# A decoder layer on one core: sixteen states of 32 channels per scan step, their sum in quarters of PSUM, and a convolution folded into four weight matrices

## The chip, the cores and the metric

The kernel runs on one core of a Trainium2 chip. A core has five engines, each with its own instruction queue that is worked in order: TensorE (PE; its weight loads are shown apart as PEld), VectorE (DVE), ScalarE (ACT), GpSimd (POOL) and SyncE (SP), which in this kernel only issues transfers. SBUF and PSUM both have 128 partitions; TensorE writes only to PSUM, which has eight banks of 512 float32 values per partition. The metric is the time of one execution on the device in microseconds (us); less is better.

## The reference, cut to what matters

Eight sequences of 256 tokens with 256 features go through three blocks, each followed by a layer norm: a Mamba block, a cross attention with a feed-forward part, and a mixture of 160 experts of which each token uses 8. The change is in the first block.

```python
xz = einsum('bld,ed->ble', x, in_proj_w)          # 256 -> 2 * 512
x_in, z = split(xz, 2)
x_c = depthwise_conv(x_in, conv_w, 4 taps, causal) + conv_b
u = silu(x_c)
dt, Bm, Cm = split(u @ x_proj_w.T, [16, 32])      # 16 values, 16 states, 16 states
delta = softplus(dt @ dt_proj_w.T + dt_proj_b)
A = -exp(A_log)                                   # 512 channels x 16 states
# over the 256 tokens of a sequence
h = h * exp(d_t[:, :, None] * A) + (d_t * u_t)[:, :, None] * b_t[:, None, :]
y = einsum('bdn,bn->bd', h, c_t)
# after the tokens
y = (y + u * D_param) * silu(z)
return y @ out_proj_w.T
```

The recurrence over h runs for 512 channels x 16 states, each over 256 tokens. All arithmetic is float32.

## The kernel before

**Stages.** The first stage (lines 173 to 711) takes the sequences one after another through the Mamba block and the attention. The second (714 to 921) sorts the tokens by expert and runs 216 blocks of 128 tokens through the experts. The third (925 to 943) gathers eight rows for each token and adds them up. The change touches the first stage alone.

**The scan loop.** The loop at line 662 has 128 steps: eight sequences b with 16 steps n. In a step of the kernel before, n is one of the 16 states, and a tile of 128 partitions x 4 x 256 holds all 512 channels (4 groups of 128) with their 256 tokens. A step has these parts:

- `product` (line 343, POOL, L348): g = du * B of state n. `du` is delta * u; the row of B is the same for all channels, so four rows at a time are read from DRAM onto all partitions (`bc_load`, L340, 512 KB).
- `decays` (L353, ACT, four instructions): exp(delta * A) of the next step, written to two PSUM tiles `decay` that exist once; they wait for the scans that still read them.
- `scans` (L363, DVE, two instructions of 512 elements): the recurrence, into the PSUM tile `states`.
- `read_out` (L372, DVE): h = states * C of state n.
- `summed` (L381, PE): two matmuls of 512 columns with the identity add h into `ya`, so that the sum over the states builds up in PSUM; in step 0 four matmuls (L384) add u * D.

**What runs beside it.** `head(b + 1)` prepares the next sequence: input projection (`pj`, L260), the convolution (one ACT instruction with the last tap, L270, and three DVE instructions for the other taps, L279, for each of the four channel groups), the z half (`sz`, L288), silu (L289, L290), `px` (L294) and `xd` (L297), `pd` (L311), softplus (L315 to L332) and `du` (L334). `rest(b - 1)` finishes the previous one: `sz` times `ya` (L400), output projection `po` (L406), keys, norm, attention, feed-forward, norms, and the routing (L561 to L622: `pl`, `pr`, `best`, `pn`, `key`).

**What sets the order.** On PE, ACT, DVE and POOL the order is the order of the program (`manual_schedule`, line 646). `head` and `rest` are generators; the loop moves each on by one piece (`go`, line 635) at fixed places of a step, and `go` always moves the oldest one of its list. Transfers on SP are ordered by the framework. A tile of a pool with `bufs=2` takes the place of the one allocated two before, and waits until that one has been read for the last time. All the PSUM results of `head` and `rest` (`bank`, line 128) come from one pool of two banks.

Of the kernel before, what the change touches and what calls it, by code (L numbers as in the profile page):

```python
# [9 lines left out]
F32 = mybir.dt.float32  # L10
AF = mybir.ActivationFunctionType
ALU = mybir.AluOpType
# [17 lines left out]
NG = 4  # L30
# [12 lines left out]
C_CONVW = 0  # L43
C_CONVB = C_CONVW + KI * NTAP
# [3 lines left out]
C_BQ = C_ALOG + KI * NS  # L48
# [14 lines left out]
def decoder_layer(  # L63
# [6 lines left out]
    in_w: bass.AP,  # L70
    xp_w: bass.AP,
# [101 lines left out]
    with ExitStack() as first:  # L173
# [3 lines left out]
        m3 = first.enter_context(tc.tile_pool(name="m3", bufs=3))  # L177
        m4 = first.enter_context(tc.tile_pool(name="m4", bufs=4))
        pools["ps"] = first.enter_context(tc.tile_pool(name="ps_front", bufs=2, space=PSUM))
# [3 lines left out]
        a2 = first.enter_context(tc.tile_pool(name="a2", bufs=2))  # L183
# [6 lines left out]

        def load_x(b):
            xt = m2.tile([P, KD, S], F32, tag="xt", name=f"xt_{b}")
            nc.sync.dma_start(xt, x_t[:, b, :].rearrange("(k p) t -> p k t", p=P))
            return xt
# [3 lines left out]
        xt0 = load_x(0)  # L198
        in_sb = weight(in_w, KD, 2 * DI, "in_sb")
# [10 lines left out]
        none = wts.tile([P, D], F32, name="none")  # L210
# [17 lines left out]
        na = wts.tile([P, KI * NS], F32, name="na")  # L228
        exps()
        nc.scalar.activation(na, cv[:, C_ALOG : C_ALOG + KI * NS], AF.Exp)  # L230
# [6 lines left out]


        decay = [held.tile([P, 2, S], F32, name=f"decay{j}") for j in range(KI // 2)]
        for t in decay:  # L240
            nc.vector.memset(t[:, :, 0:1], 0.0)
        states = held.tile([P, KI, S], F32, name="states")
        states_f = states.rearrange("p k t -> p (k t)")
# [5 lines left out]
        def head(b, xt, made):  # L249

            u = m2.tile([P, KI, S], F32, tag="u", name=f"u_{b}")
            sz = m2.tile([P, KI, S], F32, tag="sz", name=f"sz_{b}")

            def projected(j):

                pj = bank(f"pj_{b}_{j}").rearrange("p (e t) -> p e t", e=2)
                for e in range(2):
                    o = (2 * j + e) * P
                    for k in range(KD):
                        nc.tensor.matmul(  # L260
                            pj[:, e, :], in_sb[:, k, o : o + P], xt[:, k, :], start=(k == 0), stop=(k == KD - 1)
                        )
                return pj

            for j in range(KI // 2):
                pj = projected(j)
                yield
                for e in range(2):
                    k = 2 * j + e
                    nc.scalar.activation(  # L270
                        u[:, k, :], pj[:, e, :], AF.Identity, bias=cv[:, C_CONVB + k : C_CONVB + k + 1],
                        scale=cv[:, C_CONVW + (k + 1) * NTAP - 1 : C_CONVW + (k + 1) * NTAP],
                    )
                yield
                for e in range(2):
                    k = 2 * j + e
                    for i in range(NTAP - 1):
                        late = NTAP - 1 - i
                        nc.vector.scalar_tensor_tensor(  # L279
                            u[:, k, late:], pj[:, e, : S - late],  # L280
                            cv[:, C_CONVW + k * NTAP + i : C_CONVW + k * NTAP + i + 1], u[:, k, late:], ALU.mult, ALU.add,
                        )
                    if e == 0:
                        yield
            for j in range(KI // 2):
                pz = projected(KI // 2 + j)
                yield
                nc.scalar.copy(sz[:, 2 * j : 2 * j + 2, :], pz)  # L288
            nc.scalar.activation(u, u, AF.Silu)  # L289
# [6 lines left out]
            xd = m2.tile([RK + 2 * NS, S], F32, tag="xd", name=f"xd_{b}")  # L296
            nc.scalar.copy(xd, px[: RK + 2 * NS, :S])  # L297
            bc_d = dr.tile([2, NS, S], F32, tag="bc_d", name=f"bc_d_{b}")
            nc.sync.dma_start(bc_d.rearrange("a n t -> (a n) t"), xd[RK:, :])
            made["bc_d"] = bc_d  # L300
# [5 lines left out]
            delta = m2.tile([P, KI, S], F32, tag="delta", name=f"delta_{b}")  # L306
# [26 lines left out]
            du = m2.tile([P, KI, S], F32, tag="du", name=f"du_{b}")  # L333
            nc.gpsimd.tensor_mul(du, delta, u)  # L334
            made.update(u=u, sz=sz, delta=delta, du=du)

        def bc_load(b, i, n, bc_d):

            t = m2.tile([P, NG, S], F32, tag=f"bc{i}", name=f"bc{i}_{b}_{n}")
            nc.sync.dma_start(t, bc_d[i, n : n + NG, :].partition_broadcast(P))  # L340
            return t

        def product(b, n, made):

            if n % NG == 0:
                made["b_rows"] = bc_load(b, 0, n, made["bc_d"])
            g = m4.tile([P, KI, S], F32, tag="g", name=f"g_{b}_{n}")
            nc.gpsimd.tensor_mul(g, made["du"], mid(made["b_rows"][:, n % NG, :], KI))  # L348
            made[n] = g.rearrange("p k t -> p (k t)")

        def decays(b, n, made):
            for k in range(KI):
                nc.scalar.activation(  # L353
                    decay[k // 2][:, k % 2, 1:], made["delta"][:, k, 1:], AF.Exp,
                    scale=na[:, k * NS + n : k * NS + n + 1],
                )

        def scans(b, n, made):

            gf = made.pop(n)  # L360
            for j in range(KI // 2):
                part = slice(j * NT, (j + 1) * NT)
                nc.vector.tensor_tensor_scan(  # L363
                    states_f[:, part], decay[j].rearrange("p k t -> p (k t)"), gf[:, part], 0.0, ALU.mult, ALU.add
                )

        def read_out(b, n, made):

            if n % NG == 0:
                made["c_rows"] = bc_load(b, 1, n, made["bc_d"])  # L370
            h = m3.tile([P, KI, S], F32, tag="h", name=f"h_{b}_{n}")
            nc.vector.tensor_mul(h, states, mid(made["c_rows"][:, n % NG, :], KI))  # L372
            made["h"] = h.rearrange("p k t -> p (k t)")

        def summed(b, n, made, hf):

            if n == 0:
                made["ya"] = [acc.tile([P, NT], F32, tag="acc", name=f"ya_{b}_{j}") for j in range(KI // 2)]
            ya, u = made["ya"], made["u"]
            for j in range(KI // 2):  # L380
                nc.tensor.matmul(ya[j], ident, hf[:, j * NT : (j + 1) * NT], start=(n == 0), stop=(n == NS - 1))  # L381
            if n == 0:
                for k in range(KI):
                    nc.tensor.matmul(  # L384
                        ya[k // 2][:, (k % 2) * S : (k % 2 + 1) * S], diag[:, k, :], u[:, k, :],
                        start=False, stop=False,
                    )

        def rest(b, sz, ya):

            xn = a2.tile([P, TT, D], F32, tag="xn", name=f"xn_{b}")
            nc.sync.dma_start(xn, x[b].rearrange("(c p) d -> p c d", p=P))
            ct = a2.tile([P, KD, S], F32, tag="ct", name=f"ct_{b}")
            nc.sync.dma_start(ct, cx_t[:, b, :].rearrange("(k p) t -> p k t", p=P))
            cn = a2.tile([P, TT, D], F32, tag="cn", name=f"cn_{b}")
            nc.sync.dma_start(cn, cx[b].rearrange("(c p) d -> p c d", p=P))

# [24 lines left out]
            def biased(pp, bias, name):  # L422
# [592 lines left out]
```

## Time and profile before

| | before |
|---|---|
| median of 3 runs | 1525.78 us (1523.56 to 1527.69) |
| profiled execution, its own time | 1523.81 us |
| its span, first to last instruction | 1522.1 us |
| first scan starts | 44.2 us |
| h of the 128 steps | from 46.8 to 834.6 us |
| experts | from about 988 to 1336 us |
| last stage | from about 1336 us to the end |
| busy in the whole span: PE, DVE, ACT, POOL | 1125.7, 875.8, 667.5, 882.7 us |

Each row of a group gives line, engine and operation, the output and inputs by the program's names with their shapes, the number of instructions, their busy time and mean duration, and then the idle time of that engine just before them with the engine that ended it. A float32 matmul has two records on PE. The starts of h (L372) give the length of a sequence in the loop, from its step 0 to step 0 of the next: 81.1, 101.6, 108.7, 102.1, 102.6, 102.5 and 102.4 us for the sequences 0 to 6, and 86.9 us for the fifteen steps that follow step 0 of the last. A step in which DVE has nothing else takes 4.0 us.

### The profile page before, as it was taken

The numbers are of one execution on the slowest core, as the hardware profiler recorded it, in microseconds if no ns is written. First come the engines' busy times: TensorE is split into PE (matmuls) and PEld (weight loads), VectorE is DVE, ScalarE is ACT, GpSimd is POOL, SyncE is SP. The second block draws the span as 40 slices with busy tenths as digits, with TensorE's granted clock in tenths as the row PEclk, the third lists the DMA queues.
The fourth block names the chain that finished last, engine by engine and source line by source line (L and its number), as shares of the span: only waits on it lengthen the run. The fifth ranks groups of instructions, "written<-read, shape, count | busy, mean of one in ns | idle before, by whom it ended". The sixth has DMA issues, their size and how long they took to land. (4 is left out here: it accounts for less than half of the span.)

```text
span 1522.1 us, 16364 instructions
## 1 busy us (share of the span) xinstructions
PE 1125.7 (74%) x4319; PEld 747.6 (49%) x4319; DVE 875.8 (58%) x1773; ACT 667.5 (44%) x1540; POOL 882.7 (58%) x713
## 2 busy tenths in 40 slices
PE   4567688787888878877788661088888888868675
PEld 3324455455455545554455441065666666644333
DVE  2789679669777787787688218189333333310000
ACT  4375654845855757648545331022222222212222
POOL 1664365664756756847676015565666666637775
PEclk8779998889989989989889775589999999986877
DMA  8212812121212313134211000077867778634443
GB/s 274 72 47 87 295 34 67 46 62 50 50 49 57 44 47 77 42 55 44 62 29 14 21 7 8 7 226 206 245 189 215 218 228 249 191 107 134 132 135 90
DMA packets 110294, 160.20 MB, mean 105 GB/s; under 512 B 20756, under 2 KB 77622, under 8 KB 110192
## 3 DMA queue, kind: packets, MB, share of 16 engines
q1 hardware_dynamic: 77680, 114.50, 27.1%
q0 software_dynamic: 20704, 33.81, 8.3%
q10 hardware_dynamic: 11808, 10.75, 2.0%
q8 instruction: 38, 0.62, 0.2%
q14 instruction: 64, 0.52, 0.2%
HBM read 152.15 MB, written 43.58 MB: 129 GB/s over the span
## 5 line engine op out<-in xcount | busy, mean ns | idle before, releaser
L348 POOL TENSOR_TENSOR g<-du,bc 128x1024 f32<-128x1024 f32 x128 | 299.9, 2354 | 87.4 <-DVE states L363 69.9
L363 DVE TENSOR_TENSOR_SCAN states<-decay,g 128x512 f32<-128x512 f32 x256 | 314.6, 1229 | 58.7 <-ACT decay L353 25.9
L353 ACT ACTIVATE decay<-delta,na 128x255 f32<-128x255 f32 x512 | 238.0, 474 | 130.1 <-DVE states L363 119.2
L830 POOL DMA_INDIRECT xg<-x_d,tokens x216 | 216.0, 1000 | 131.6 <-PE bt L841 121.9
L381 PE MATMUL ya<-h,ident 128*128 128x512 f32 x512 | 264.0, 648 | 29.9 <-DVE h L372 29.9
L843 DVE COPY bx<-bt 128x256 f32<-128x256 f32 x216 | 91.5, 424 | 180.6 <-PE bt L841 179.6
L852 PE MATMUL by<-we,bg 128*128 128x256 f32 x432 | 151.3, 432 | 44.5 <-ACT bg L850 36.8
L381 PEld LDWEIGHTS ya<-h,ident 128*128 128x128 f32 x512 | 102.3, 208 | 135.2 <-issue 78.7
L850 ACT ACTIVATE bg<-bh 128x128 f32<-128x128 f32 x216 | 59.8, 277 | 247.7 <-PE bh L846 243.2
L372 DVE TENSOR_TENSOR h<-states,bc 128x1024 f32<-128x1024 f32 x128 | 156.2, 1220 | 7.9
L628 POOL DMA_INDIRECT tab_d<-pair_no,placei x128 | 130.7, 1021 | 42.0 <-issue 30.0
L934 POOL DMA_INDIRECT y<-y_d,sloti x128 | 121.0, 945 | 58.4 <-issue 35.3
L940 PE MATMUL yn<-y,diags 128*128 128x256 f32 x256 | 110.8, 551 | 42.4 <-DMA y<-y_d,sloti 41.3
L846 PEld LDWEIGHTS bh<-bx,we 128*128 128x128 f32 x864 | 130.0, 193 | 20.2 <-DVE bx L843 8.2
L846 PE MATMUL bh<-bx,we 128*128 128x128 f32 x864 | 134.7, 279 | 4.1 <-DVE bx L843 2.8
L852 PEld LDWEIGHTS by<-we,bg 128*128 128x128 f32 x432 | 65.2, 189 | 96.7 <-ACT bg L850 96.2
L940 PEld LDWEIGHTS yn<-y,diags 128*128 128x128 f32 x256 | 56.2, 257 | 94.8 <-DMA y<-y_d,sloti 90.0
L941 DVE TENSOR_TENSOR xs<-xs,yn 128x512 f32<-128x512 f32 x8 | 5.5, 688 | 158.1 <-PE yn L940 158.1
L524 PE MATMUL ph<-x2t,w_sb 128*128 128x256 f32 x256 | 71.9, 443 | 31.6 <-ACT x2t L512 31.2
L841 PE MATMUL bt<-ident,xg 128*128 128x128 f32 x432 | 83.5, 275 | 3.8 <-DMA xg<-x_d,tokens 3.8
L524 PEld LDWEIGHTS ph<-x2t,w_sb 128*128 128x128 f32 x256 | 56.3, 225 | 51.3 <-ACT x2t L512 37.0
L260 PE MATMUL pj<-xt,in_sb 128*128 128x256 f32 x256 | 65.7, 403 | 17.6 <-DMA in_sb<-in_in_w_dram 8.3
(220 smaller groups left out, 1609.9 us busy)
## 6 DMA issues: line engine op xcount, KB each, us to landing
we<-in_experts_dram SPq DMA_DIRECT2D x216, 256.0 KB, 3.4
bc<-bc_d SPq DMA_DIRECT2D x64, 512.0 KB, 5.7
y_d<-bo SPq DMA_DIRECT2D x216, 128.0 KB, 3.0
y_d<-none ACTq DMA_DIRECT2D x1, 9216.0 KB, 31.4
xg<-x_d,tokens POOLq DMA_INDIRECT x216, 3.6
xt<-in_x_t_dram SPq DMA_DIRECT2D x8, 256.0 KB
w_sb<-in_w_dram SPq DMA_DIRECT2D x2, 1024.0 KB, 10.9
xn<-in_x_dram SPq DMA_DIRECT2D x8, 256.0 KB, 5.2
```

The source lines that it names most:

```text
L348: nc.gpsimd.tensor_mul(g, made["du"], mid(made["b_rows"][:, n % NG, :], KI))
L353: nc.scalar.activation(decay[k // 2][:, k % 2, 1:], made["delta"][:, k, 1:], AF.Exp, scale=na[:, k * NS + n : k * NS + n + 1],)
L363: nc.vector.tensor_tensor_scan(states_f[:, part], decay[j].rearrange("p k t -> p (k t)"), gf[:, part], 0.0, ALU.mult, ALU.add)
L372: nc.vector.tensor_mul(h, states, mid(made["c_rows"][:, n % NG, :], KI))
L381: nc.tensor.matmul(ya[j], ident, hf[:, j * NT : (j + 1) * NT], start=(n == 0), stop=(n == NS - 1))
L524: nc.tensor.matmul(ph[:, i, :], w1_sb[:, k, f * P : (f + 1) * P], x2t[:, k, :], start=(k == 0), stop=(k == KD - 1),)
L628: nc.gpsimd.indirect_dma_start(out=tab_views[i * TOPK + j], out_offset=bass.IndirectOffsetOnAxis(ap=placei[:, c, j : j + 1], axis=0), in_= ...
L830: nc.gpsimd.indirect_dma_start(out=xg[i % LANES], out_offset=None, in_=x3_d, in_offset=bass.IndirectOffsetOnAxis(ap=tokens[:, i : i + 1], ...
L846: nc.tensor.matmul(ph, w[:, k * P : (k + 1) * P], xt[:, k * P : (k + 1) * P], start=(k == 0), stop=(k == KD - 1))
L852: nc.tensor.matmul(py, g, w[:, KD * P :], start=True, stop=True)
L934: nc.gpsimd.indirect_dma_start(out=y8[:, j, :], out_offset=None, in_=y_d, in_offset=bass.IndirectOffsetOnAxis(ap=sloti[:, i, j : j + 1], a ...
L940: nc.tensor.matmul(pn[:, c, :], diags[:, i, j, :], y8[:, j, :], start=False, stop=(j == TOPK - 1))
```

## The change: what it does

**Scan steps.** A step now holds 32 channels with all their 16 states: partition r * 32 + i holds channel i of the 32, and the four groups g of the free axis the states 4g + r. The scan, the product, the decays and h keep their shapes. B and C, rearranged, are read once for each sequence (`rows_of`, four transfers each). What now differs from step to step is delta and du, which must lie on all four quarters of the partitions: `head` writes delta and delta * u to a DRAM tile `spread_d`, and `spread` reads them back for two steps at a time, four transfers of 64 KB for each of the two.

**Sum.** The sum over the states is now partly over partitions. `summed` runs once for four steps, with 16 matmuls of 256 columns whose stationary operand `over` (128 x 32, four stacked identities) adds the four quarters up; each of the four steps goes to its own 32 partitions of `ya`.

**Convolution.** in_proj_w of the x half is multiplied by each of the four taps once at the start (`tap_w`, two on DVE, two on POOL), and a channel group of `pj` is eight matmuls on an input that is shifted by 0 to 3 tokens. The convolution's DVE instructions are gone.

**Pacing and buffers.** `head` starts at step 2 and moves on twice a step, and is finished by step 10; `rest` spreads its first two pieces over steps 0 and 1, and moves on up to six times a step while two are unfinished. h has five buffers, g four; several other tiles have one buffer instead of two.

```diff
+        tap_w = [wts.tile([P, KD, DI], F32, name=f"tap_w{i}") for i in range(NTAP)]
+        for i in range(NTAP):
+            eng = (nc.vector, nc.gpsimd)[i % 2]
+            eng.tensor_mul(tap_w[i], in_x, mid(taps[i // 2][:, i % 2, :], KD))
...
             for j in range(KI // 2):
                 pj = bank(f"pj_{b}_{j}").rearrange("p (e t) -> p e t", e=2)
+                for e in range(2):
+                    o = (2 * j + e) * P
+                    for i in range(NTAP):
+                        for k in range(KD):
+                            nc.tensor.matmul(
+                                pj[:, e, :], tap_w[i][:, k, o : o + P], xt[:, k, i : i + S],
+                                start=(i == 0 and k == 0), stop=(i == NTAP - 1 and k == KD - 1),
+                            )
+                    yield
+                for e in range(2):
+                    k = 2 * j + e
+                    nc.scalar.activation(
+                        u[:, k, :], pj[:, e, :], AF.Identity, bias=cv[:, C_CONVB + k : C_CONVB + k + 1]
+                    )
...
-                        nc.vector.scalar_tensor_tensor(
-                            u[:, k, late:], pj[:, e, : S - late],
-                            cv[:, C_CONVW + k * NTAP + i : C_CONVW + k * NTAP + i + 1], u[:, k, late:], ALU.mult, ALU.add,
-                        )
...
-            du = m2.tile([P, KI, S], F32, tag="du", name=f"du_{b}")
-            nc.gpsimd.tensor_mul(du, delta, u)
+            spread_d = dr.tile([2, DI, S], F32, tag="spread_d", name=f"spread_d_{b}")
+            nc.sync.dma_start(spread_d[0].rearrange("(k p) t -> p k t", p=P), delta)
+            nc.gpsimd.tensor_mul(v, delta, u)
+            nc.sync.dma_start(spread_d[1].rearrange("(k p) t -> p k t", p=P), v)
...
+        def spread(b, j, made):
+
+            both = []
+            for a, name in enumerate(("spread_delta", "spread_du")):
+                t = m3.tile([P, 2, S], F32, tag=name, name=f"{name}_{b}_{j}")
+                for r in range(NR):
+                    nc.sync.dma_start(
+                        t[r * CH : (r + 1) * CH],
+                        made["spread_d"][a, 2 * j * CH : 2 * (j + 1) * CH, :].rearrange("(q i) t -> i q t", i=CH),
+                    )
+                both.append(t)
...
+            h = m5.tile([P, NG, S], F32, tag="h", name=f"h_{b}_{n}")
+            nc.vector.tensor_mul(h, states, made["bc"][1])
...
-            for j in range(KI // 2):
-                nc.tensor.matmul(ya[j], ident, hf[:, j * NT : (j + 1) * NT], start=(n == 0), stop=(n == NS - 1))
...
+            hs = [made.pop(("h", k * NR + q)) for q in range(NR)]
+            for g in range(NG):
+                for q in range(NR):
+                    nc.tensor.matmul(
+                        made["ya"][k // 2][q * CH : (q + 1) * CH, (k % 2) * S : (k % 2 + 1) * S], over, hs[q][:, g, :],
+                        start=False, stop=(g == NG - 1), skip_group_check=True, tile_position=(0, q * CH),
+                    )
...
+                if n == 2:
+                    skipped(b, made)
+                    if b + 1 < B:
+                        heads.append(head(b + 1, rows_made[b + 1]))
+                if n % NR == 0 and i > 0:
                     b0, n0 = steps[i - 1]
-                    summed(b0, n0, rows_made[b0], rows_made[b0]["h"])
-                if n % 2 == 0:
-                    go(heads)
+                    summed(b0, n0 // NR, rows_made[b0])
+                go(heads)
                 read_out(b, n, made)
```

## The prediction

> **What bounds the kernel now.** I read the slices first, then the groups and the waits, then DVE's and PE's order of time through one sequence of the scan loop.
>
> ```profile
> PE   4567688787888878877788661088888888868675
> DVE  2789679669777787787688218189333333310000
> ```
> ```profile
> L363 DVE TENSOR_TENSOR_SCAN states<-decay,g 128x512 f32<-128x512 f32 x256 | 314.6, 1229 | 58.7 <-ACT decay L353 25.9
> L381 PE MATMUL ya<-h,ident 128*128 128x512 f32 x512 | 264.0, 648 | 29.9 <-DVE h L372 29.9
> L372 DVE TENSOR_TENSOR h<-states,bc 128x1024 f32<-128x1024 f32 x128 | 156.2, 1220 | 7.9
> ```
>
> The loop fills slices 2 to 22 (44 to 836 us). No engine is full there: in the stretch from 530 to 628 us PE is busy 79.3 of 98 us, DVE 78.7, ACT 64.6, POOL 63.0. Two scans and an h cost DVE 4.0 us a step, 64 of the 102.5 us of a sequence; the rest is the side work of `head` and `rest`, and waits. With four queues worked in order, what counts is which is late at which place.
>
> ```profile
> 540.02 0.30 DVE L145 BATCH_NORM_AGGREGATE mv_x<-st_x 128x2 f32<-128x6 f32 x2
> 554.30 0.33 DVE L577 MAX8 best<-pr 128x8 f32<-128x160 f32 x1 [3.87 <-ACT pr L567]
> 570.80 0.68 DVE L430 TENSOR_TENSOR xn<-xn,po 128x512 f32<-128x512 f32 x1
> 572.39 1.49 DVE L279 SCALAR_TENSOR_TENSOR u<-pj,cv,u 128x253 f32<-128x253 f32 x3
> 600.92 1.23 DVE L372 TENSOR_TENSOR h<-states,bc 128x1024 f32<-128x1024 f32 x1
> ```
> ```profile
> 525.51 7.07 PE L535 MATMUL pf<-w_sb,ht 128*128 128x256 f32 x32
> 532.42 3.17 PE L381 MATMUL ya<-h,ident 128*128 128x512 f32 x7
> ```
> ```profile
> ACT u L270 <- PE pj L260: 39.5, 10, 9.2
> PE pkt L417 <- DVE xn L430: 18.6, 6, 6.4
> ```
>
> I count from T0 = 540.3, where the last norm's statistics end. `best` comes 14.0 later, held by a chain through ACT and PE; the h after nine scans starts at T0 + 60.6; the next T0 is 102.5 later. PE's rate when full: 32 records of 256 columns from 525.51 to 532.42, 0.216 us each, and a float32 matmul has two records (512 for 256 in L381), so **0.43 us a matmul**, and 1.72 for a step's two of 512 columns. The waits show two things the change will meet: ACT stops at `u` until PE has finished `pj`, and PE stops because a PSUM bank of the two is held until DVE reaches `xn`.
>
> **The change part by part.**
>
> *DVE.* Four `x3` rows like the one at 572.39 go: 4 x 1.5 = 6.0 us a sequence, 42 for the seven heads inside the loop. Scan, h, product and decays keep shape and price.
>
> *PE.* `pj` grows from 8 to 32 matmuls: 24 x 0.43 = +10.3 us a sequence. The sum falls from 16 x 1.72 = 27.5 us to four bursts of 16 matmuls, S each. No matmul on a quarter of the columns is in the trace. Bounds: no overlap of the quarters, 16 x 0.43 = 6.9; all four at once, 1.7. I take two at once, **S = 3.4**, since neighbours in the program use different quarters but the two records of one matmul use the same. All in all PE's work falls by 3.4 us, but it moves: `pj` comes as 32 matmuls between steps 2 and 4, just when `rest` is densest, and the sum waits behind it in PE's queue.
>
> The Trainium skill ("TensorE: Matmul & The Clock Gate", Part 3) gives three column tiles side by side a measured gain of 2.38; by it four would give an estimated 3.2 and S about 2.2, and the total would be some 10 us lower; no trace here shows it.
>
> *A steady sequence, from T0, in the new program order.* `best` at 14.0 as before. Its operations to the reciprocal (2.4), h 1.3 and `sz` x `ya` 1.3 end at 18.9; `key` to the weights 5.6, 24.5; scans and h 3.9, 28.4; `xn` ends at 29.1. Meanwhile `po` and `pkt` hold both banks, so `pj` starts only here. PE: 16 `pj`, 4 `pv`, 16 `pj` in two halves, that is 36 x 0.43 + 0.5 for transposes = 16.0, 45.1. The next bank is that of `pj`, so `pqt` waits for ACT's `u` (1.1), 46.3, and takes 1.7, 48.0. The burst ends at 48.0 + S = 51.4. DVE is through scan 5 at 43.0, but h 5 needs the buffer of h 0, which the burst frees: **DVE waits 8.4 us**, and with it every scan behind. After the burst come `pz` and `psc` on PE; ACT's decays for scan 6 stand behind `sz`, and end at 55.6; scan 6 runs to 58.2. The probabilities then stand behind `sz` 0.6, two table loads 2.6, two silus 2.1, a table load 1.3 less what overlaps, 0.2 and 0.9, and end at 63.0, so DVE waits again, 4.8 us; h 6 and scan 7 follow, and h 7 starts at 67.1, after as many scans as the 60.6 of before: **+6.5**. The rest of the sequence keeps its order and its known waits (41.5 by the same walk, 41.9 in the trace, -0.4), but h 13 needs the second-last burst, which stands behind `pf`: +1.7. Sum **+7.8 us a sequence**; that is 110.3. For sequences 3 to 6, 4 x 7.8 = 31.2. Sequence 2, which took 108.7, gets +2; sequence 1 has no routing of an earlier `rest` in front, took 101.6 and comes out equal; sequence 0 loses 6.0 and waits for `pj` and for the chain of silu and softplus, -1 by the same walk; the last has no head: 0. What runs after the loop is as before.
>
> *The start.*
>
> ```profile
> 8.26 5.62 PE L260 MATMUL pj<-xt,in_sb 128*128 128x256 f32 x16 [8.26 <-DMA in_sb<-in_in_w_dram]
> 20.86 0.58 ACT L288 COPY sz<-pj 128x512 f32<-128x512 f32 x1 [2.08 <-PE pj L260]
> 37.54 1.23 DVE L332 SCALAR_TENSOR_TENSOR delta<-v,delta 128x1024 f32<-128x1024 f32 x1 [3.57 <-POOL delta L329]
> 44.20 2.57 DVE L363 TENSOR_TENSOR_SCAN states<-decay,g 128x512 f32<-128x512 f32 x2 [5.43 <-POOL g L348]
> ```
>
> Before the first `pj` now come 1.75 MB instead of 1.3, so about 9 us; the last `tap_w` ends at 11, hidden by the first matmuls. 32 `pj` and 8 `pz` are 80 records; with the first eight at half rate they take 3.5 + 72 x 0.216 = 19.1 and end at 28.1, the second `sz` at 28.7 instead of 21.4: **+7.3**. From there to delta nothing changes. From delta (38.8) to the first scan took 5.4. Now: product delta * u 2.35; its 512 KB to DRAM, 0.4 to issue and 5.0 to land (256 KB of x_d land in 4.3, 512 KB of bc in 5.7); four loads of 64 KB, 4 x 0.32 to issue and 2.6 for the last (256 KB of cn); product 2.36: 14.0, **+8.6**. Later in the loop the same trip is covered: delta ends about 84 us after T0, the next sequence's first scan is at 114.
>
> *SP.* 64 transfers of 512 KB become 512 of 64 KB and 64 for B and C: 84 issues in a sequence x 0.32 = 27 us of 110, and each pair is asked for three steps before its product. The two writes of `spread_d` wait for DVE and POOL, and behind them stand only loads that need them. I cost this at nothing; the cover is those three steps, 19 us.
>
> "DMA: Bandwidth & Descriptors" (Rules for kernel authors) of the Trainium skill speaks against it: transfers under 64 KB are mostly overhead, to be made into large ones. The rows agree that size hardly counts, 32 KB of bc_d land in 4.6 us; by the rule the loads would cost their latency, and the sum would stay as long as they overlap.
>
> **Sum.** 1523.8 + 15.9 + 31.2 + 2 - 1 = 1571.9: **1572 us**, against the profiled execution, 2.0 below the median. A measurement of this kernel tells 0.3% from no change, 4.6 us.
>
> **The rivals.**
>
> *DVE still sets the pace.* Then each head's 6.0 us are won: 1523.8 - 42 + 15.9 = **1498**. For it: PE's work falls, and DVE is the engine whose work goes. Against: the order. It decides at one point: the first burst would have to end by T0 + 43, 13.9 us after `xn`, while what stands ahead of it takes 18.9. With half of the gain it is a draw.
>
> *The quarters do not overlap*, S = 6.9. The first burst costs 3.5 more, the second 3.5 more, and the last, before `pn`, some 3: +17.8 a sequence. Four of these 71, sequence 2 +11, sequence 1 +5, sequence 0 -1 and the start 15.9: **1626**. For it: nothing in the trace shows two matmuls at once. Against: the addresses are disjoint.
>
> *The loads come too late.* With no overlap, eight of 2.6 us are 20.8 for a pair, against 13.7 us for two steps: +7 x 64, about 1970. Against: the start's transfers are issued 0.5 us apart and do overlap. Two in flight are enough.
>
> **How the numbers follow.** Forecast 0.55, its own range 1545 to 1605 (S of 1.7 gives 1558; 4 us a sequence for errors of the walk); DVE's pace 0.20; no overlap 0.21; late loads 0.04. The range, 1503 to 1628, leaves out about half of DVE's pace, half of no overlap, and late loads. Faster by over 0.3%: most of DVE's pace and a corner of the forecast, 0.21; within 0.3% 0.07; slower 0.72.
>
> **What would show it.** In the new profile: first scan near 60 us; sequences 3 to 6 near 110; DVE's h waiting some 8 us for PE's sum once a sequence; `pj` on PE starting when `xn` ends, and ACT's `u` behind it; a burst of 32 records in 3.4 us. The prediction is wrong if h never waits for PE, if `pj` starts before `xn`, or if a sequence takes under 100.

## The result, and the profile after

| | before | after |
|---|---|---|
| median of the undisturbed runs | 1525.8 us (1523.56 to 1527.69) | **1578.4 us** (1577.51 to 1578.93) |
| span of the profiled execution | 1522.1 us | 1576.4 us |
| first h | 46.8 us | 61.5 us |
| sequences 0 to 6 | 81.1, 101.6, 108.7, 102.1, 102.6, 102.5, 102.4 | 83.9, 101.9, 108.0, 108.1, 109.1, 109.7, 109.1 |
| last fifteen steps | 86.9 us | 87.4 us |
| last h to the router's last count (`total`, L728 / L783 on PE) | 91.2 us | 89.4 us |
| from there to the first expert matmul (`bh`) | 65.9 us | 78.6 us |
| from there to the end | 530.3 us | 529.8 us |

The change makes the kernel slower: ratio 1.0345, 95% interval 1.0327 to 1.0363. The stretches of the table add up to the 54.3 us between the spans: +14.7 for the start, +29.3 for the steps, and +10.3 after the loop.

The slices of the page after, in the same form as before (busy tenths of 40 equal slices):

```profile
PE   5354976858669668768667562048888888876776
DVE  2469478587586675784878516169533333310000
```

The groups of the page after (line, engine, operation and shapes, count, then busy time and mean ns, then the idle time just before and what ended it):

```profile
L394 DVE TENSOR_TENSOR_SCAN states<-decay,g 128x512 f32<-128x512 f32 x256 | 314.7, 1229 | 79.5 <-ACT decay L385 39.5
L401 DVE TENSOR_TENSOR h<-states,bc 128x1024 f32<-128x1024 f32 x128 | 156.3, 1221 | 52.9 <-PE ya L419 46.4
L282 PE MATMUL pj<-xt,tap_w 128*128 128x256 f32 x512 | 122.1, 397 | 21.4 <-ACT early L462 11.8
L419 PE MATMUL ya<-h,over 128*32 128x256 f32 x1024 | 88.2, 470 | 27.7 <-DVE h L401 27.6
```

Scan and h cost what they did. The sum fell from 264.0 to 88.2 us, and PE's whole busy time from 1125.7 to 1091.4, DVE's from 875.8 to 841.0. Two engines have less to do, and the kernel is slower: the idle time before h went from 7.9 to 52.9 us, and 46.4 of it now ends with PE's sum. The granted TensorE clock over the steps fell as well. These are windows from the first h to the last, of the kernel before and then of the changed one (stretch, its length, busy us of PE, PEld, DVE, ACT and POOL with instructions, granted clock, DMA share, GB/s):

```profile
46.80:834.60 787.80, 622.50 (x2028) 392.15 (x2028) 623.41 (x821) 487.30 (x1039) 485.23 (x296) 0.90 0.26 64
61.50:878.60 817.10, 580.08 (x2859) 417.53 (x2860) 587.66 (x742) 488.64 (x1046) 486.38 (x296) 0.78 0.34 82
```

In the same stretch of e1 below, which has the new scan layout without the new convolution, the clock is 0.78 too, and in e2, which has the convolution alone, it is 0.92. So the lower clock goes with the new layout. What it costs in all, no run separates.

The waits of the whole run point to PE as well (engine, line and what it waited for: us in total, times, longest):

```profile
ACT u L289 <- PE pj L282: 61.5, 15, 16.0
DVE h L401 <- PE ya L419: 46.4, 14, 6.8
DVE states L394 <- ACT decay L385: 39.5, 15, 4.1
DVE total L513 <- ACT early L508: 31.7, 7, 5.1
```

In time order the place is sequence 4, whose T0 (end of the last norm's statistics) is 456.8. First PE's timeline (start, us, instructions, and idle time before in brackets), then two rows of ACT's and three of DVE's:

```profile
482.01 1.89 PE L408 MATMUL ya<-u,diag 128*128 128x256 f32 x8
486.32 8.86 PE L282 MATMUL pj<-xt,tap_w 128*128 128x256 f32 x32 [2.42 <-ACT early L462]
495.02 1.89 PE L476 MATMUL pv<-attn_w,ct 128*128 128x256 f32 x8
496.75 3.62 PE L282 MATMUL pj<-xt,tap_w 128*128 128x256 f32 x16
500.64 3.62 PE L282 MATMUL pj<-xt,tap_w 128*128 128x256 f32 x16
504.10 1.89 PE L452 MATMUL pqt<-x1t,attn_w 128*128 128x256 f32 x8
505.92 1.93 PE L419 MATMUL ya<-h,over 128*32 128x256 f32 x32
```
```profile
484.52 0.99 ACT L385 ACTIVATE decay<-spread_delta,na 128x255 f32<-128x255 f32 x2 [0.28 <-DVE states L394]
485.45 0.82 ACT L462 ACTIVATE early<-pkt,cv 128x256 f32<-128x256 f32 x2
```
```profile
485.67 0.68 DVE L467 TENSOR_TENSOR xn<-xn,po 128x512 f32<-128x512 f32 x1
507.87 1.23 DVE L401 TENSOR_TENSOR h<-states,bc 128x1024 f32<-128x1024 f32 x1 [6.79 <-PE ya L419]
511.54 0.69 DVE L503 TENSOR_REDUCE top<-psc 128x2 f32<-128x512 f32 x1 [2.45 <-PE psc L496]
```

Some 20 us of PE work stand between `xn` and the burst of the sum (505.92), 16 of them the shifted in_proj. h 5 needs the buffer that the burst frees and waits 6.8 us; `top` and the probabilities come behind it in the same queue.

### The profile page after: what moved, and what is told of

Same layout as the page of the kernel before. It is cut to its first block, busy times and chain, and to the rows that moved or that the text cites. A ratio compares the mean times of both kernels' runs of the same rounds, so it can differ in the third digit from the quotient of the medians.

```text
span 1576.4 us, 18977 instructions
## 1 busy us (share of the span) xinstructions
PE 1091.4 (69%) x5215; PEld 780.4 (50%) x5215; DVE 841.0 (53%) x1683; ACT 666.4 (42%) x1540; POOL 889.6 (56%) x715
## 5 line engine op out<-in xcount | busy, mean ns | idle before, releaser
L379 POOL TENSOR_TENSOR g<-bc,spread_du 128x1024 f32<-128x1024 f32 x128 | 299.9, 2355 | 104.4 <-DVE states L394 84.4
L394 DVE TENSOR_TENSOR_SCAN states<-decay,g 128x512 f32<-128x512 f32 x256 | 314.7, 1229 | 79.5 <-ACT decay L385 39.5
L385 ACT ACTIVATE decay<-spread_delta,na 128x255 f32<-128x255 f32 x512 | 238.6, 474 | 178.7 <-DVE states L394 143.5
L401 DVE TENSOR_TENSOR h<-states,bc 128x1024 f32<-128x1024 f32 x128 | 156.3, 1221 | 52.9 <-PE ya L419 46.4
L282 PE MATMUL pj<-xt,tap_w 128*128 128x256 f32 x512 | 122.1, 397 | 21.4 <-ACT early L462 11.8
L282 PEld LDWEIGHTS pj<-xt,tap_w 128*128 128x128 f32 x512 | 101.1, 200 | 39.1 <-ACT early L462 13.8
L419 PE MATMUL ya<-h,over 128*32 128x256 f32 x1024 | 88.2, 470 | 27.7 <-DVE h L401 27.6
L561 PEld LDWEIGHTS ph<-x2t,w_sb 128*128 128x128 f32 x256 | 59.5, 238 | 52.0 <-ACT x2t L549 38.4
```

The source lines that it names most:

```text
L282: nc.tensor.matmul(pj[:, e, :], tap_w[i][:, k, o : o + P], xt[:, k, i : i + S], start=(i == 0 and k == 0), stop=(i == NTAP - 1 and k == KD ...
L379: nc.gpsimd.tensor_mul(g, made["bc"][0], mid(made["spread"][n // 2][1][:, n % 2, :], NG))
L385: nc.scalar.activation(decay[g // 2][:, g % 2, 1:], delta[:, n % 2, 1:], AF.Exp, scale=na[:, n * NG + g : n * NG + g + 1])
L394: nc.vector.tensor_tensor_scan(states_f[:, part], decay[j].rearrange("p g t -> p (g t)"), gf[:, part], 0.0, ALU.mult, ALU.add)
L401: nc.vector.tensor_mul(h, states, made["bc"][1])
L561: nc.tensor.matmul(ph[:, i, :], w1_sb[:, k, f * P : (f + 1) * P], x2t[:, k, :], start=(k == 0), stop=(k == KD - 1),)
```

## The experiments

Different chips were in use. On those that ran e5 to e8 and e12 the kernel before took 1558.8 and 1557.8 us; from its first expert matmul to the end, e5 takes 562.8 us where the changed kernel took 529.8 on its own, while the scan steps take as long. So every ratio is to the kernel before on the same chip, and traces are compared by the time of the router's last count, which closes the first stage.

| kernel | first h | mean of sequences 3 to 6 | last count at | ratio to before |
|---|---|---|---|---|
| before | 46.8 | 102.4 | 925.9 | 1 |
| after | 61.5 | 109.0 | 968.1 | 1.0345 [1.0327, 1.0363] |
| e1 conv on DVE | 51.9 | 106.5 | 939.5 | 1.0141 [1.0115, 1.0167] |
| e2 before, conv on PE | 55.6 | 104.5 | 948.5 | 1.0164 [1.0142, 1.0187] |
| e3 quarters in turn | 63.7 | 114.0 | 1010.8 | 1.0640 [1.0610, 1.0669] |
| e4 six h buffers | 61.4 | 111.7 | 978.7 | 1.0446 [1.0412, 1.0480] |
| e5 head one step early | 61.4 | 109.3 | 968.0 | 1.0391 [1.0371, 1.0411] |
| e6 half the loads | 66.8 | 113.1 | 994.6 | 1.0495 [1.0477, 1.0513] |
| e7 conv on DVE, half the loads | 57.5 | 109.3 | 959.0 | 1.0246 [1.0228, 1.0263] |
| e8 conv on DVE, early head | 51.8 | 106.2 | 938.4 | 1.0143 [1.0125, 1.0162] |
| e9 kt before the decays | 64.0 | 106.4 | 953.8 | 1.0236 [1.0214, 1.0257] |
| e10 head spaced | 65.0 | 109.4 | 976.2 | 1.0384 [1.0366, 1.0401] |
| e11 both | 61.7 | 108.8 | 965.0 | 1.0312 [1.0284, 1.0340] |
| e12 both, evenly | 61.7 | 111.1 | 975.7 | 1.0405 [1.0367, 1.0443] |

**e1: the convolution back on DVE, the rest of the change kept.**

```diff
-                    for i in range(NTAP):
-                        for k in range(KD):
-                            nc.tensor.matmul(pj[:, e, :], tap_w[i][:, k, o : o + P], xt[:, k, i : i + S], ...)
+                    for k in range(KD):
+                        nc.tensor.matmul(pj[:, e, :], in_x[:, k, o : o + P], xt[:, k, NTAP - 1 :], ...)
...
+                        nc.vector.scalar_tensor_tensor(u[:, k, late:], pj[:, e, : S - late], ..., ALU.mult, ALU.add)
```

> The changed kernel with the convolution alone undone: one matmul per tap set (8 instead of 32 for pj), the last tap on ACT and twelve tap instructions a sequence on DVE again. Theory A (the 24 extra matmuls, issued between xn and the first burst of the sum, hold h 5 and the decays; the new layout is free in the loop): PE reaches the burst some 12 us earlier after xn, the three waits there (h for the burst 6.8, scan for decay 2.9, top for psc 2.5) go, DVE gets 6.0 us of taps: a sequence takes 109.1 - 12.2 + 6.0 = 103, and the first scan comes some 8 us earlier, near 51 us: 1578 - 8 - 5 x 6 = about 1540. Theory B (the new layout with its trip through DRAM costs the loop time): sequences stay at 109 or rise by the 6.0 of the taps, 1570 to 1605.

1549.0 us: some 59% of the loss goes with the convolution (1.0141 against 1.0345). h's waits for the sum fall from 46.4 to 4.0 us. Of the 26.1 us that stay between the spans, 5.1 lie at the start, 10.1 in the steps and 10.9 after the loop. In the steps the way through DRAM shows. POOL's waits from 60 to 891 us:

```profile
POOL g L383 <- DMA spread_du<-spread_d: 45.5, 6, 19.7
```

The product waits six times for its load, four of them at the end of a sequence, and step 14 takes 4.7 to 10.4 us in sequences 2 to 6, some 15 us more in all than the 4.7 a step of the changed kernel. But these waits are probably e1's own: with the taps back its head has two pieces more, and delta * u leaves for DRAM in step 12 instead of step 10. In the changed kernel the convolution's part of the loss in the steps is then larger than e1 shows; no run tells how large.

**e2: the kernel before with its convolution on TensorE**, and of the rest of the change only the shared buffers that make room for it.

```diff
+                        for i in range(NTAP):
+                            for k in range(KD):
+                                nc.tensor.matmul(pj[:, e, :], tap_w[i][:, k, o : o + P], xt[:, k, i : i + S], ...)
-                        nc.vector.scalar_tensor_tensor(u[:, k, late:], pj[:, e, : S - late], ..., ALU.mult, ALU.add)
```

> The kernel before with the convolution alone moved to TensorE, in the same pieces and at the same places of a step; kt, qt, val and prob share the place of ht, and xt and xd exist once, as in the changed kernel, to make room for tap_w. Theory A (the extra matmuls cost more than the taps because PE's queue is then late): first scan at 44.2 + 8 = 52 us; PE's 10.3 us come on top of 84 busy us, DVE loses 6.0: sequences of 102.5 become about 106, in all about 1526 + 8 + 5 x 4 = 1554. Theory B (DVE paces the loop, so that taking 6.0 us from it is a gain): sequences of 97 to 98, 1526 + 8 - 35 = about 1499.

1551.1 us: moving 6 us a sequence from DVE to PE loses here as well, without any new layout. `xn` waits 14.1 us for PE's `po` instead of 5.5, and `best` 41.1 us for ACT's `pr` instead of 25.1; ahead of `pr` in ACT's queue stands `u`, which waits 112.6 us for PE's `pj` instead of 39.5. Both begin with something late on PE; whether the shared buffers add to the loss was not tried. The spans of e1 and e2 lie 26.1 and 22.2 us over that of before, together 48.3, the whole change 54.3: the two halves nearly add up, with 6 us left over (by the medians 45.4 and 52.6).

**e3: the four quarters one after another.**

```diff
-            for g in range(NG):
-                for q in range(NR):
+            for q in range(NR):
+                for g in range(NG):
```

> The changed kernel with the two loops of the summing matmuls exchanged, so that four matmuls in a row go to the same quarter; the same 16 matmuls. Theory A (the four quarters overlap, which is why 32 records take 1.93 us): without overlap a burst takes 16 x 0.43 = 6.9 us; the first and second burst of a sequence that DVE waits for cost 5 us each, the last one before pn some 3: 12 a sequence, sequences near 121, about 1578 + 6 x 12 = 1650. Theory B (the overlap is only in how the ends of matmuls are modelled): no change, 1578.

Three bursts of one sequence on PE's timeline (granted clock 0.66 of full speed in the first, 1.00 in the others):

```profile
484.94 6.81 PE L419 MATMUL ya<-h,over 128*32 128x256 f32 x32
523.01 4.59 PE L419 MATMUL ya<-h,over 128*32 128x256 f32 x32
551.15 4.59 PE L419 MATMUL ya<-h,over 128*32 128x256 f32 x32
```

4.59 us instead of 1.93, with the same matmuls: the overlap of neighbours in different quarters is real, and worth 44 us to the kernel (1622.5). But in turn they don't take the 6.9 us of 16 matmuls of 0.43 either, so the loss is smaller than the 72 us I expected. A side effect softens it too: with q outermost, h 0 is read for the last time after four matmuls, so h 5 still waits 6.8 us and the rest shows later, in `top` and in the decays.

**e4: six h buffers instead of five**, paid for in SBUF with `PAIRS` 3 instead of 4.

```diff
-PAIRS = 4
+PAIRS = 3
...
-        m5 = first.enter_context(tc.tile_pool(name="m5", bufs=5))
+        m5 = first.enter_context(tc.tile_pool(name="m5", bufs=6))
```

> The changed kernel with six buffers of h instead of five, and three instead of four pairs of steps loaded ahead, to make room. h 5 no longer waits for the first burst; h 6 does. Theory A (the buffer only shows a lateness of PE that ACT's decays and psc have as well): scan 6 still waits for the decays behind sz, which ended 4.4 us after h 5 could start: a gain of 1 to 2.5 us a sequence, 1565 to 1572, and nothing lost by loading three pairs ahead instead of four. Theory B (too few h buffers are the cause): the 6.8 us of each sequence are won, 1578 - 7 x 6.8 = about 1530.

1592.6 us. Steps 4 and 5 of sequence 4 took 7.4 + 18.7 = 26.1 us where the changed kernel took 14.1 + 12.0 = 26.1. The buffer is only the place at which PE's lateness shows first; with a sixth, DVE runs into the next thing that PE makes (DVE's waits from 360 to 800 us):

```profile
DVE top L503 <- PE psc L496: 36.8, 4, 9.2
```

What it lost on top (14.2 us) fits the loads, three pairs ahead instead of four: in sequences 2 to 6 step 14 takes 4.9 to 9.1 us instead of 4.7 to 5.4, some 13 us in all. With two things changed at once, e4 shows where a sixth buffer moves the wait, not what it is worth by itself.

**e5: the head one step earlier**, so that half of `pj_0` stands ahead of `po`.

```diff
-                    if b + 1 < B:
-                        heads.append(head(b + 1, rows_made[b + 1]))
...
+                if n == 1 and b + 1 < B:
+                    heads.append(head(b + 1, rows_made[b + 1]))
```

> The changed kernel with one move: the next sequence's head starts at the end of step 1 instead of in step 2, so that the first half of its shifted in_proj (half of pj_0, 16 of 64 matmul records) stands ahead of po and kt in TensorE's queue, where TensorE waits for the router's key chain of VectorE, and every later piece of the head moves up by one place. Theory A (pj behind xn is what makes TensorE late at step 5): pj behind xn shrinks from 8.86 us to some 4.5, the second burst and the score products come 4 us earlier, h's wait of 6.8 falls to 2 to 3 and top's from 2.5; a sequence 104 to 106 instead of 109, 1545 to 1562 us. Rival B: TensorE's place in the queue is not it, but the bank that the head holds: po then waits for the other bank, which the key chain frees, xn comes later by as much, and nothing is won: 1573 to 1590.

The count comes at 968.0, as in the changed kernel: nothing won, so rival B's result, and by a mechanism near its own: `po` doesn't wait for a bank, but `kt` now waits for `xn`. PE's timeline:

```profile
488.89 1.99 PE L454 MATMUL pkt<-ct,attn_w 128*128 128x256 f32 x8 [2.07 <-DVE xn L469]
```

`xn` ends at T0 + 29.6 as before. `pz_0` moved up into the place that half of `pj_0` had left ahead of the burst, which starts at T0 + 50.6 instead of 49.2; and ACT's copy of `pj` moved up with it and stands ahead of the decays, so that the scan waits at step 3 (DVE's timeline):

```profile
497.86 2.56 DVE L396 TENSOR_TENSOR_SCAN states<-decay,g 128x512 f32<-128x512 f32 x2 [4.31 <-ACT decay L387]
```

**e6 and e7: half as many loads, each twice as large**, in the changed kernel and in e1's.

```diff
-                for r in range(NR):
-                    nc.sync.dma_start(t[r * CH : (r + 1) * CH], made["spread_d"][a, ...].rearrange("(q i) t -> i q t", i=CH))
+                for q in range(2):
+                    src = made["spread_d"][a, (2 * j + q) * CH : (2 * j + q + 1) * CH, :]
+                    nc.sync.dma_start(t[:, q, :], bass.AP(..., ap=[[0, NR]] + [list(x) for x in src.ap]))
```

> The changed kernel with the loads of the spread delta and product in two transfers of 128 partitions each instead of four of 32 (the repeat of the four quarters is in the source's pattern): four issues for a channel pair instead of eight, the same bytes. Theory A (the prediction's: the loads lie hidden behind four pairs of lead): no change, 1573 to 1583 us. Rival C (the sync queue is long enough in issuing, 128 transfers a sequence, that loads or weights of the next stage come late): 10 to 25 us less.

> The changed kernel with the convolution back on VectorE (1549 us measured) and the loads in half as many transfers. There the product waits at step 14 for the next sequence's first pair (45.5 us in 6 waits). Theory D (that pair is late because the head ends late; the issue itself takes 1.7 us for four): 0 to 8 us less, 1541 to 1549. Rival C (it is late because the sync queue is busy): 20 us or more less, 1530 or under.

Theory A and rival C of e6, and theory D and rival C of e7, are all wrong: slower, by 1.5% and 1.0% of the kernel before. Two stretches of the start, first SP's timeline of the changed kernel, then of e6, in which SP issues load after load without any other wait (the second number is the time that it takes to issue them), and then a window over each:

```profile
57.14 1.83 SPq L369 DMA_DIRECT2D spread_du<-spread_d  x4
59.02 1.83 SPq L369 DMA_DIRECT2D spread_delta<-spread_d  x4
```
```profile
65.23 2.66 SPq L370 DMA_DIRECT2D spread_du<-spread_d  x2
67.93 2.57 SPq L370 DMA_DIRECT2D spread_delta<-spread_d  x2
```
```profile
59.00:63.00 4.00, 0.00 (x0) 0.00 (x0) 3.86 (x4) 1.91 (x4) 4.00 (x2) 0.50 0.48 136
62.00:70.00 8.00, 0.00 (x0) 0.00 (x0) 5.62 (x4) 1.92 (x4) 6.65 (x3) 0.50 0.27 93
```

SP issues 256 KB in 1.83 us as four transfers of 32 partitions, and in 2.66 us as two of 128 partitions; meanwhile the data move at 136 and at 93 GB/s. From the first du load's issue to the product it was 3.5 us (52.96 to 56.50), and in e6 6.2 (55.67 to 61.87). Step 14 then takes 7 to 11.5 us in sequences 2 to 6 instead of 4.7 to 5.4. So the loads are not free in the changed kernel; they are just in time.

This does not settle the advice of the Trainium skill that the prediction weighed ("DMA: Bandwidth & Descriptors", Rules for kernel authors), to make small transfers into large ones, since e6 changed the pattern together with the size. Its outermost dimension is the repeat of four, and the DMA share of 0.27 means that on average 4.3 of the 16 DMA engines were busy (0.27 x 16), where the changed kernel had 7.7. Larger transfers in another pattern were not run.

**e8: e1 with the head one step earlier** (the same edit as e5, on e1).

> The changed kernel with the convolution back on VectorE and the head started at the end of step 1 instead of in step 2, so that its last piece, the write of delta and of the product to DRAM, comes at the end of step 9 instead of in step 10. Theory D (the pair is late because the head ends late): the waits at step 14 fall by some 5 us each, a sequence 100 to 103, 1520 to 1538 us. Rival C (the sync queue): no change, 1544 to 1553.

1.0143, no change, and inconclusive: the write of delta left at 521.95 us, in e1 at 522.08. The edit moved the last piece by half a step at most, and delta * u still left in step 12, so the run decides between neither theory.

**e9: kt's copies on ACT ahead of the decays of step 3.**

```diff
             pk = projected(wk, ct, "kt")
+            kt = biased(early[:, 0], pk, C_BK)
             yield
             nc.vector.tensor_add(xn, xn, po)
-            kt = biased(early[:, 0], pk, C_BK)
...
-                if i + 1 < len(steps):
+                if i + 1 < len(steps) and n != 2:
                     decays(*steps[i + 1], rows_made[steps[i + 1][0]])
                 go(rests)
...
+                if i + 1 < len(steps) and n == 2:
+                    decays(*steps[i + 1], rows_made[steps[i + 1][0]])
```

> The changed kernel with one move on ScalarE: the copies of kt out of PSUM stand ahead of the decays of step 3 instead of behind them. In the changed kernel's trace the shifted in_proj begins at the end of those copies (486.32 after 486.27), which stand in ScalarE's queue behind decays that wait for the scan of step 2, behind the router's key chain; kt itself had left TensorE at 482.2, and TensorE was idle for 2.42 us. Theory A (what holds pj is the PSUM bank of kt, not xn as the prediction had it; xn ends at the same moment by chance): pj starts 2.4 us sooner and without the pause in front, at a higher clock; h's wait at step 5 falls from 6.8 to 3 to 4.4, a sequence 105 to 107 instead of 109, ratio to the kernel before 1.017 to 1.027 instead of 1.0345. Rival B (xn or the key chain holds the rest as well): ratio 1.031 to 1.037.

1564.4 us, 1.0236: theory A, though h's wait at step 5 is still 5.6 us in sequence 4, not 3 to 4.4. Sequence 4 has T0 at 452.4. PE's timeline and then DVE's:

```profile
476.06 1.89 PE L452 MATMUL pkt<-ct,attn_w 128*128 128x256 f32 x8
479.52 7.07 PE L282 MATMUL pj<-xt,tap_w 128*128 128x256 f32 x32
497.32 1.93 PE L419 MATMUL ya<-h,over 128*32 128x256 f32 x32
```
```profile
481.25 0.68 DVE L468 TENSOR_TENSOR xn<-xn,po 128x512 f32<-128x512 f32 x1
499.27 1.23 DVE L401 TENSOR_TENSOR h<-states,bc 128x1024 f32<-128x1024 f32 x1 [5.63 <-PE ya L419]
```

The windows of the changed kernel and of e9 over the first matmuls of `pj` (in the form of the first two windows):

```profile
486.30:491.00 4.70, 4.68 (x14) 3.86 (x15) 4.53 (x8) 3.49 (x11) 3.71 (x4) 0.65 0.19 52
491.00:495.00 4.00, 4.00 (x19) 3.49 (x19) 3.76 (x5) 0.28 (x1) 1.24 (x1) 0.99 0.59 125
```
```profile
479.50:483.00 3.50, 3.50 (x18) 3.05 (x17) 3.43 (x8) 1.32 (x4) 2.68 (x2) 1.00 0.09 28
```

`pj` now starts before `xn`, at T0 + 27.2 instead of 29.6, and without a pause ahead of it the clock stays at 1.00: its 32 records take 7.07 us instead of 8.86. The burst starts at T0 + 45.0 instead of 49.2, 4.2 us sooner, by a copy of 0.8 us that no longer stands behind the decays. h's wait falls by only 1.2 us, because the scan before it no longer waits 2.9 us for its decays, and DVE comes to h 5 sooner too; h 5 itself starts 4.2 us sooner. The sequences took 103.6, 110.1, 104.9 and 106.8; the one of 110.1 lost 3.3 us more at step 14, where the product waited 3.4 us for its load.

**e10, e11, e12: the head's pieces spread out**, so that the burst and the scores stand ahead of half of the shifted in_proj. e10 does it with one piece in steps 2 and 3 and three in steps 7 and 8; e11 adds e9's move; e12 is e11 with the third piece in step 7 alone.

```diff
-                go(heads)
+                if n not in (2, 3):
+                    go(heads)
+                if n in (7, 8):
+                    go(heads)
```

> The changed kernel with one piece of the next head instead of two in steps 2 and 3, made up for in steps 7 and 8: TensorE's order becomes half of pj_0, pv, half of pj_0, x1's transposes, qt, the burst of the sum, half of pj_1, the scores, half of pj_1 (in the changed kernel all of pj_0 and pj_1, some 16 us, stands ahead of qt, the burst and the scores). Theory A (the sum costs through its place behind the whole shifted in_proj): the burst and the scores come 4 to 7 us sooner, h no longer waits at step 5, a sequence 101 to 105, ratio 1.0 to 1.018. Rival B (TensorE's work between xn and the probabilities is what counts, in whatever order, or the head's end comes late and the product waits at step 14): 107 to 111 a sequence, ratio 1.025 to 1.04.

> Both moves together. Theory A: they add up, since the one moves the start of pj and the other what stands behind it: a sequence 99 to 103, ratio 0.99 to 1.01. Rival B: once h doesn't wait, the chain through x1's norm sets the pace, and the second move takes up the first one's gain: the same as the better of the two alone, within 0.3%.

> Both moves again, with the head's postponed pieces made up for by a single piece more in step 7, so that delta's chain (exp, log, the subtraction on GpSimd) is no longer crowded into step 8, where its steps of 13.4 us instead of 7.1 paid back the 4 to 6 us won at step 4. Theory A (the shifted in_proj costs through what stands behind it in TensorE's queue, and the only thing that spoiled the spacing was delta's crowded end): step 4 stays at 5.4 to 7, step 8 falls to 7 to 9, a sequence 100 to 104, ratio 1.000 to 1.018. Rival B (the head's chain from u to the loads is itself as long as the time it is given, so a later start is paid at its end wherever the pieces are put): the waits come back at step 9 or at step 14, ratio 1.02 to 1.032.

The lengths of some steps of sequence 5 (us, from the starts of h):

| step | 3 | 4 | 5 | 6 | 7 | 8 | 9 | 12 | 14 | sequence |
|---|---|---|---|---|---|---|---|---|---|---|
| after | 3.9 | 12.4 | 12.0 | 3.9 | 12.4 | 7.1 | 4.0 | 6.8 | 4.7 | 109.7 |
| e5 | 9.8 | 11.4 | 10.8 | 4.7 | 8.8 | 4.9 | 4.0 | 8.5 | 5.0 | 109.4 |
| e9 | 3.9 | 9.6 | 12.0 | 3.9 | 11.4 | 7.1 | 4.0 | 6.8 | 4.7 | 104.9 |
| e10 | 3.9 | 6.5 | 10.9 | 5.0 | 10.7 | 13.4 | 4.0 | 7.2 | 4.7 | 108.8 |
| e11 | 3.9 | 5.4 | 11.0 | 5.0 | 10.7 | 13.4 | 4.0 | 6.8 | 4.7 | 107.3 |
| e12 | 3.9 | 5.4 | 11.0 | 5.0 | 10.7 | 7.4 | 8.6 | 8.0 | 7.0 | 109.1 |

Theory A was right about the place and wrong about the sum. Against the changed kernel step 4 falls by 6 to 7 us, as expected, though in e10 h still waits 3.9 us at step 5 (sequence 4); but the 6 us come back at step 8 (e10, e11), or at steps 9, 12 and 14 (e12). e10's ratio is the one that rival B gave. e11's fits neither theory: it is not as good as e9, the better of its two moves alone. e12's waits are where rival B put them, and its ratio is above even that range. DVE's waits of e12 from 360 to 800 us, and then POOL's timeline around the load:

```profile
DVE st_x L148 <- POOL x L581: 15.5, 4, 5.2
DVE delta L348 <- POOL delta L345: 14.4, 4, 3.6
```
```profile
569.29 2.34 POOL L379 TENSOR_TENSOR g<-bc,spread_du 128x1024 f32<-128x1024 f32 x1 [5.38 <-DMA spread_delta<-spread_d]
```

From the start of `pj` to the write of delta it is 54.7 us in the changed kernel (486.32 to 541.07), 54.9 in e9, and 57.5 in e10 and in e12: the head goes by its pieces in the steps. This fits two bounds that lie close together, PE's queue up to the burst, and the head with its trip through DRAM, so that relieving the first by more than e9 does runs into the second. No version beat the kernel before; e9 is the best with the whole change in it.

## Why the prediction was right, and where its steps were off

**The verdict and its mechanism held.** h waits for PE's sum once a sequence, the burst stands behind the shifted in_proj, and less work on DVE and on PE made the loop longer. The rival "DVE still sets the pace" had the right condition: the burst would have had to end by T0 + 43; it ended at T0 + 51.1; in e9, where it ended at T0 + 46.9, a sequence of 3 to 6 lost 4.0 us instead of 6.6.

**The walk through a sequence.** `xn` ended at T0 + 29.6 (forecast 29.1), h 5 waited 6.8 us (8.4), the probabilities 5.1 (4.8), h 7 started at T0 + 67.0 (67.1). Sequences 3 to 6 cost 26.4 us more than before instead of 31.2.

**S was mis-sized.** Taken as 3.4 us, between 1.7 and 6.9; it measured 1.93 at a granted clock of 1.00 and 3.64 at 0.50. All four quarters work side by side, and not two at a time: 1.93 us is close to the bound of 1.7. With that the second-last burst behind `pf` costs nothing where 1.7 us were put down. It did not save more at the first burst because in sequence 4 `pj` took 8.86 us for its first 32 records, where 6.9 were forecast from the rate when full; the two errors nearly cancel up to h 7, so that the match there is in part luck. The walk has PE at its full rate throughout, while the granted clock over the steps was 0.78. The rival "quarters do not overlap" had its price of 1626 from S = 6.9; e3 shows that even one quarter in turn takes 4.59, and got to 1622.5 by other ways.

**`pj` and `xn`.** The step "both banks are held, so `pj` starts only here" put the right time on the wrong cause. By the order in which the tiles are asked for, `pj` would take the bank of `po`, which `xn` reads. But it takes that of `kt`, and that one waits for copies on ACT behind two decays; in the changed kernel they end 0.1 us before `xn` does, and `pj` starts 0.05 us after them. e9 moves the copies alone, and `pj` starts 1.7 us before `xn` does.

**The start.** +14.7 us against 15.9: the convolution's part is 8.3 (7.3 forecast; the second `sz` copy ends at 29.8), the trip's part 6.3 (8.6): delta to the first scan 11.8 instead of 14.0.

**The loads at nothing.** Right for the changed kernel, where step 14 takes 4.7 us; but the cover of "three steps, 19 us" was counted from the request of a pair within a sequence. Where two sequences meet, the request stands behind the write of delta * u, and little slack is left: e9, which leaves the head's pieces in their places, waits there for 3.4 us once, and e4, e6 and e12 wait there in most sequences. How large the slack is was not measured.

**What was left out.** "What runs after the loop is as before" is wrong by 10.3 us, the largest error of the sum. The loss is in the stretch from the router's last count to the first expert matmul, in which POOL writes the routing table for the last two sequences. Three rows of POOL's timeline after, and the last of them as it was before:

```profile
990.00 0.96 POOL L665 DMA_INDIRECT tab_d<-pair_no,placei  x1 [3.30 <-DMA tab_d<-pair_no,placei]
999.57 0.96 POOL L665 DMA_INDIRECT tab_d<-pair_no,placei  x1 [8.61 <-DMA tab_d<-pair_no,placei]
1033.18 1.03 POOL L846 DMA_INDIRECT got<-tab_d,rowi  x1 [10.63 <-DMA tab_d<-pair_no,placei]
```
```profile
977.96 1.03 POOL L791 DMA_INDIRECT got<-tab_d,rowi  x1 [6.00 <-DMA tab_d<-pair_no,placei]
```

The same 32 indirect writes are issued, and with the read behind them they wait some 14 us longer for earlier ones of their own kind (26.0 us instead of 12.0), while nothing else of size moves: the DMA share is 0.02 in both. The stretch took 65.9 us before and 66.3 in e2; in the changed kernel and the eleven others with its layout (e1, e3 to e12) 78 to 83. So it comes with the new layout (its buffers and pacing included) and not with the convolution. Why was not tried and stays open.

**The sum.** 1571.9, less 1.2 for the start, less 4.8 for sequences 3 to 6, plus 1.9 for the other steps (forecast +1, measured +2.9), plus 10.3 after the loop: 1578.1, the time of the profiled execution. The forecast was 6.2 us under it, with errors of both signs.

## What to carry to other kernels

Where engines work fixed queues, price a moved operation by what stands behind it at that place, not by the busy time of the engine it came from: 6 us of DVE work became 10 us of PE work in the one stretch in which the other engines wait for PE. Before adding a buffer, ask what the producer delivers next; before taking a wait's releaser for its cause, look for another that ended at the same moment, and move one of them alone. And a chain through DRAM needs its slack counted where it is shortest, here from the last sequence's write to the next one's first product.

## What the runs showed of the hardware that I had not expected

- Sixteen float32 matmuls of 256 columns on 32 output partitions each take 1.93 us when neighbours use the four quarters and 4.59 when four in a row use the same one. By the 0.216 us of a full-width record they would take 6.9. Why the same quarter in turn beats that rate as well is open; their weight loads are shorter too, 118 ns on average in e3 (130 with the quarters mixed) instead of the 200 of `pj`.
- A short pause of PE can be followed by a lower clock, at a price beside that of the pause. In the changed kernel `pj` comes behind a pause in five sequences: after 2.63, 2.42 and 2.58 us its first 32 records took 8.86 us (granted clock of 0.65 over the first 4.7 us in sequence 4), after 1.83 and 2.35 us they took 7.18. In e9, without the pause, they took 7.07 each time.
- A load that spreads 32 rows over 128 partitions from one transfer (128 KB, the repeat of four outermost in its source) takes SP about 1.3 us to issue, with a DMA share of 0.27; four transfers of 32 partitions (256 KB together) take 1.83, with a share of 0.48.
